# Four-layer graph network: another order in layer 2's loop, and its one-hot matrices made on ScalarE

## The chip, the cores and the metric

The kernel runs on one core of one Trainium2 chip. The metric is the device time of one execution in microseconds (us), given as the median of several runs. A profile of one further execution gives the times of single instructions. The engines are named as in the profile: PE is TensorE, PEld its weight loads, DVE is VectorE, ACT is ScalarE, POOL is GpSimd, and SP is the engine that issues most plain DMAs.

## The reference

There are 12500 nodes with 128 features and 212500 edges, sorted by destination. Four layers follow one another. Each normalises the node features, takes the positive part, gathers a row for the source of every edge, forms a message, sums the messages by destination and adds the result to the features. Layer 2, the third of them, is the one that changes. Its message is a tensor product of the source's features with nine numbers of the edge, cut to what matters:

```
PATHS = [(0, 0, 0), (0, 1, 1), (1, 0, 1), (1, 1, 0), (1, 2, 1)]
x1 = _split(features[src], IRREPS_IN)      # 32 scalars, 32 vectors of 3
x2 = _split(edge_sh, IRREPS_SH)            # 1 + 3 + 5 numbers an edge
for p, (i1, i2, io) in enumerate(PATHS):
    tmp = jnp.einsum('eui,ej,ijk->euk', x1[i1], x2[i2][:, 0, :], CG[p])
    msg = jnp.einsum('euk,uw->ewk', tmp, weights[p]) * alpha
    out_blocks[io] = msg if out_blocks[io] is None else out_blocks[io] + msg
...
return out.at[dst].add(msgs)
h = jnp.maximum(_layernorm(x, axis=-1), 0.0)
x = x + _L2_gnn_ref(h, edge_attr_9, edge_index, L2_gnn_weights)
```

## The kernel before

Edges are handled in groups of 1024: 8 slices (t = 0 to 7) of 128 edges, one edge to a partition, so that there are 208 groups (NG) in each layer. The destinations of a group lie within a window of 128 nodes. The sum over edges is a matmul: the message tile is the stationary operand and a one-hot tile is the moving one, with a 1 where edge and window node belong together. `rel` holds for every edge its destination's place in the window, 0 to 127, and `iop` holds 0 to 127 along the free dimension, in PSUM. The running sums stand in `acc`, features by nodes, in SBUF.

Layer 2 keeps an order written out by hand: under `tc.manual_schedule()` every engine executes its instructions in the order in which the program issues them, and semaphores only make them wait. One iteration of the loop takes one group g into the pipeline:

- `rows2` gathers the 8 slices of X from the table `htab` by 8 indirect DMAs, which POOL issues (L629 inside `gather`). X has 11 buffers.
- `mix(g + 1)` makes the edge factors Y ("harmonics") of the next group: a transposition on PE (L1129), its copy `eT` on ACT (L1131), a product with `mixer` on PE (L1132). Every fourth call also loads a batch of edge numbers `ef` through SP, and the last batch has a memset on POOL in it (L131).
- `window2` is a generator. Each `step(k)` drives group k's generator on to its next `yield`. The parts are: first A, the features times the first edge number, in 8 ACT instructions (L1142); second the one-hot S in one DVE instruction (L644 inside `one_hot`); third the products B and C in 8 DVE instructions (L1149 to L1161); fourth the sums `pag` over edges on PE in three blocks A, B and C (L1167), with two ACT copies to R (L1169, L1170); fifth the product `po` with the weights on PE (L1174); sixth the addition to `acc` on DVE (L1177).

Within iteration g the order is: `nodes.step`, gather g, A of g, `mix(g + 1)`, one-hot of g, addition of g-3, products of g, sums and copies of g-1, `po` of g-2. So ACT executes A(g), eT(g+1), R(g-1); PE executes the transposition and mixing of g+1, the sums of g-1, `po` of g-2; DVE executes the one-hot of g, the addition of g-3, the products of g.

`nodes` finishes blocks of 4 times 128 nodes (`node2`, 25 blocks) once their sums are complete: transpositions of `acc` on PE (L498), then normalisation on DVE and ACT, and stores through SP. They start at iteration `done + 4`, one iteration after the addition of the block's last group.

The matmuls are in float32, which the profile shows as two matmul and two weight-load instructions each: 16 for 8 slices.

Of the kernel before, what the change touches and what calls it, by code (L numbers as in the profile page):

```python
# [12 lines left out]
F = mybir.dt.float32  # L13
I = mybir.dt.int32
B16 = mybir.dt.bfloat16
AF = mybir.ActivationFunctionType
# [8 lines left out]
P = 128  # L25
T = 8
GE = P * T
W = 128
# [62 lines left out]
def gnn_kernel(ctx: ExitStack, tc, x, src, dst, ef16, ef9, ew, W0, We0, a0, lns, lnb, W1, b1,  # L91
# [6 lines left out]
    NG = NF + (tail > 0)  # L98
# [15 lines left out]
    vec, act, pool, pe = nc.vector, nc.scalar, nc.gpsimd, nc.tensor  # L114
# [59 lines left out]
    iop = cps.tile([P, W], F, name="iop")  # L174
# [3 lines left out]
    ones = cst.tile([P, P], F, name="ones")  # L178
# [294 lines left out]
    def node1(sp, pp, k):  # L473
        b0, nb = k * NBK, min(NBK, NB - k * NBK)
        xv = sp.tile([P, nb, D], F, name="xv")
        load_rows(xv, xtab[0], b0, nb)
        g = sp.tile([P, nb, P], F, name="g")
        act.activation(g.rearrange("p j n -> p (j n)"), acc[:, cols(k)], AF.Gelu_apprx_tanh)
        yield
        vec.memset(acc[:, cols(k)], 0.0)  # L480
        po = pp.tile([P, nb, D], F, name="pn")
        for j in range(nb):
            pe.matmul(po[:, j, :], g[:, j, :], W1T, start=True, stop=True)
        yield
        o = sp.tile([P, nb, D], F, name="o")
        vec.tensor_tensor(o, po, b1_b[:, None, :].to_broadcast([P, nb, D]), ALU.add)
        act.activation(o, o, AF.Gelu_apprx_tanh)
        yield
        vec.tensor_tensor(xv, xv, o, ALU.add)
        yield from keep(sp, 1, k, xv, True)  # L490
# [121 lines left out]
    class Nodes:  # L612
# [5 lines left out]
        def step(self, g):  # L618

            while self.next < NK and done[self.next] + self.delay <= g:  # L620
                self.going.append(self.make(self.next))
                self.next += 1
            self.going = [w for w in self.going if next(w, "end") != "end"]
            return self.going or self.next < NK
# [16 lines left out]
    def one_hot(sp, r, wgt=None, dt=F):  # L641
        s = sp.tile([P, T, W], dt, name="oh")
        if wgt is None:
            vec.tensor_tensor(s, iop[:, None, :].to_broadcast([P, T, W]), r[:, :, None].to_broadcast([P, T, W]),  # L644
                              ALU.is_equal)
        else:
            for t in range(T):
                vec.tensor_scalar(s[:, t, :], io, r[:, t : t + 1], wgt[:, t : t + 1], op0=ALU.is_equal, op1=ALU.mult)  # L648
        return s
# [109 lines left out]
    with (tc.tile_pool(name="e0", bufs=2) as sp, tc.tile_pool(name="e0p", bufs=2, space=PSUM) as pp,  # L759
# [106 lines left out]
        def spread_out(g):  # L866

            X, ev = xs.pop(g), alphas.pop(g)
            S = sp.tile([P, T, W], F, name="oh")
            vec.tensor_tensor(S, iop[:, None, :].to_broadcast([P, T, W]),  # L870
                              rel[:, g, :, None].to_broadcast([P, T, W]), ALU.is_equal)
# [5 lines left out]
            for t in range(T):  # L877
                pe.matmul(pag[:, 0, :], msg[:, t, :], S[:, t, :], start=t == 0, stop=t == T - 1)  # L878
            for t in range(T if g < G0 else 0):
                pe.matmul(pag[:1, 1, :], ones[:, :1], S[:, t, :], start=t == 0, stop=t == T - 1)  # L880

# [9 lines left out]
        with tc.manual_schedule():  # L891
# [4 lines left out]
            g = -1  # L896
# [193 lines left out]
    with (tc.tile_pool(name="e1", bufs=3) as sp, tc.tile_pool(name="e1p", bufs=2, space=PSUM) as pp,  # L1090
          tc.tile_pool(name="n1", bufs=2) as ns, tc.tile_pool(name="n1p", bufs=1, space=PSUM) as np_,
          tc.tile_pool(name="so", bufs=2) as ss, tc.tile_pool(name="sop", bufs=1, space=PSUM) as sps):
        reg = Window(DVE, True)
        S, pags, X = {}, {}, {}
        nodes = Nodes(lambda k: node1(ns, np_, k), 3)
        slots = Slots(ss, sps)
        with tc.manual_schedule():
            g = -1
            while nodes.step(g := g + 1) or g < NG + 2:
                if g < NG:  # L1100
                    X[g] = gather_apart(sp, htab[0], si[:, g, :], 12 * T)
                    S[g] = one_hot(sp, rel[:, g, :], eww[:, g, :])
                if 0 <= g - 2 < NG:
                    win = ds(reg.load(bi[0:1, g - 2 : g - 1]), W)
                    reg.end(vec.tensor_tensor(acc[:, win], acc[:, win], pags.pop(g - 2), ALU.add))  # L1105
                if 0 <= g - 1 < NG:
                    p = pags[g - 1] = pp.tile([P, W], F, name="pag")
                    s, r = S.pop(g - 1), X.pop(g - 1)
# [8 lines left out]
    def layer2(sp, pp, deep=4):  # L1117
        feats = feature_stream(ef9f, 9, 4, "ef", sp)

        def rows2(idx):  # L1120
            X = sp.tile([P, T, P], F, name="X", bufs=deep)
            gather(X, htab[1], idx)
            return X

        def mix(g):

            e = feats(g)
            py = pp.tile([P, 2, P], F, name="py")
            pe.transpose(py[: T * 9, 0, :], e, ident)  # L1129
            eT = sp.tile([T * 9, P], F, name="eT")  # L1130
            act.copy(eT, py[: T * 9, 0, :])  # L1131
            pe.matmul(py[:, 1, : T * NY], eT, mixer, start=True, stop=True)  # L1132
            return e.rearrange("p (t k) -> p t k", k=9), py[:, 1, : T * NY].rearrange("p (t k) -> p t k", k=NY)

        def stream2(g, idx, wgt):
            return rows2(idx), *mix(g)

        def window2(reg, got, r, b, nodes):
            X, e, Y = got
            A = sp.tile([P, T, P], F, name="A")  # L1140
            for t in range(T):
                act.activation(A[:, t, :], X[:, t, :], AF.Copy, scale=e[:, t, 0:1])  # L1142
            yield
            S = one_hot(sp, r)
            yield
            x1 = X[:, :, HD:].rearrange("p t (k u) -> p t k u", k=3)
            v3 = [P, T, 3, HD]
            B = sp.tile([P, T, 4, HD], F, name="B")
            vec.tensor_tensor(B[:, :, :3, :], X[:, :, None, :HD].to_broadcast(v3),  # L1149
                              Y[:, :, 0:3, None].to_broadcast(v3), ALU.mult)  # L1150
            V = pp.tile(v3, F, name="part", bufs=1)
            vec.tensor_tensor(V, x1, Y[:, :, 12:15, None].to_broadcast(v3), ALU.mult)  # L1152
            vec.tensor_reduce(B[:, :, 3, :], V.rearrange("p t k u -> p t u k"), AX.X, ALU.add)
            C = sp.tile(v3, F, name="C")
            part = pp.tile(v3, F, name="part", bufs=1)
            for i in range(3):
                o = part if i == 0 else sp.tile(v3, F, name="term", bufs=1)
                vec.tensor_tensor(o, x1[:, :, i : i + 1, :].to_broadcast(v3),  # L1158
                                  Y[:, :, 3 + 3 * i : 6 + 3 * i, None].to_broadcast(v3), ALU.mult)
                if i:  # L1160
                    vec.tensor_tensor(part if i == 1 else C, part, o, ALU.add)  # L1161
            yield
            pag = pp.tile([P, 3, W], F, name="pag", bufs=1)
            for c, f in enumerate((A, B, C)):
                for t in range(T):
                    lhs = f[:, t] if c == 0 else f[:, t].rearrange("p k u -> p (k u)")
                    pe.matmul(pag[: TPK[c] * HD, c, :], lhs, S[:, t, :], start=t == 0, stop=t == T - 1)  # L1167
            R = sp.tile([P, 3, W], F, name="R")
            act.copy(R[:, :2, :], pag[:, :2, :])  # L1169
            act.copy(R[: 3 * HD, 2, :], pag[: 3 * HD, 2, :])  # L1170
            yield
            po = pp.tile([P, W], F, name="po", bufs=1)
            for c, k in enumerate(TPK):
                pe.matmul(po, TP[: k * HD, c, :], R[: k * HD, c, :], start=c == 0, stop=c == 2)  # L1174
            yield
            win = ds(reg.load(b), W)
            reg.end(vec.tensor_tensor(acc[:, win], acc[:, win], po, ALU.add))  # L1177

        return rows2, mix, stream2, window2

    with (tc.tile_pool(name="e2", bufs=3) as sp, tc.tile_pool(name="e2p", bufs=2, space=PSUM) as pp,
          tc.tile_pool(name="n2", bufs=2) as ns, tc.tile_pool(name="n2p", bufs=1, space=PSUM) as np_):
        rows2, mix, _, window2 = layer2(sp, pp, 11)
        nodes = Nodes(lambda k: node2(ns, np_, k), 4)
        reg2, mixed, going = Window(DVE, True), {}, {}

        def step(k):
            if k in going:
                next(going[k], None)

        with tc.manual_schedule():
            mixed[0] = mix(0)
            g = -1
            while nodes.step(g := g + 1) or g < NG + 3:
                if g < NG:
                    going[g] = window2(reg2, (rows2(si[:, g, :]), *mixed.pop(g)), rel[:, g, :],
                                       bi[0:1, g : g + 1], widx[:, g : g + 1])
                    step(g)
                if g + 1 < NG:
                    mixed[g + 1] = mix(g + 1)  # L1200
                step(g)
                step(g - 3)
                step(g)
                step(g - 1)
                step(g - 2)

# [107 lines left out]
    with tc.tile_pool(name="l3", bufs=1) as lp:  # L1314
        stats = lp.tile([P, NK, 6], F, name="stats")
        with (tc.tile_pool(name="t3", bufs=1) as tp, tc.tile_pool(name="e3", bufs=2) as sp,
# [9 lines left out]
            X, S, sums, flat3, going = {}, {}, {}, {}, []  # L1326
# [3 lines left out]
            with tc.manual_schedule():  # L1330
# [9 lines left out]
                g, count, nk, alive = -1, 0, 0, True  # L1340
                while g < G0 + 8 or alive or going or waiting:
# [21 lines left out]
                    if 0 <= h < G0:  # L1363
                        p = sums[h] = pp.tile([P, 3 * P], F, name="pg")
                        s, r = S.pop(h), X.pop(h)
# [213 lines left out]
```

## Time and profile before

| | us |
|---|---|
| median of 3 runs | 10488.28 (10479.12 to 10490.92) |
| the profiled execution | 8214.33 |
| its span, first to last instruction | 8212.6 |
| layer 2 in it, about 4536 to 6841 | 2305 |

The profiled execution is shorter than the runs by 2274 us; nothing in the profile shows that time. The granted PE clock was 0.718 of full speed over the span.

To read the page: a group's line has source line, engine, operation, output and inputs with their shapes and count, then busy time and mean duration, then the idle time of the engine before the group's instructions, with what ended most of it. In a timeline line there are start, length, engine, source line, operation, count, and in brackets the idle time before it with its releaser. POOL's 8 gathers of a group are separate instructions.

### The profile page before, as it was taken

Reading aid. Unit: us, or ns where it says so; the run is one execution under the profiler, and the core shown is the slowest. Engines: PE = TensorE matmul, PEld = TensorE weight load, DVE = VectorE, ACT = ScalarE, POOL = GpSimd, SP = SyncE. Lnnn points to the kernel's source line nnn. Section 1 sums busy time; section 2 is a strip of 40 time slices with the busy share of each in tenths; the row PEclk is TensorE's granted clock in tenths of the full one; section 3 lists DMA queues with packets and bytes.
Section 4 is the critical chain, followed back from the end, with each engine's and each line's share of the span. In section 5 each row is a group of like instructions: output and inputs, shape, how many; then the busy total and the mean of one; then the engine's idle time right before and its main releaser. Section 6 shows DMA issues by size and latency. Waiting matters only on the chain. (4 is left out here: it accounts for less than half of the span.)

```text
span 8212.6 us, 100482 instructions
## 1 busy us (share of the span) xinstructions
PE 5336.5 (65%) x32201; PEld 3954.0 (48%) x32202; DVE 5348.6 (65%) x10674; ACT 1691.6 (21%) x4403; POOL 5718.1 (70%) x6026
## 2 busy tenths in 40 slices
PE   3455555544446666666666677777777775877786
PEld 2344444444434444444444677777777772222222
DVE  6466666666666666556562788888888883444444
ACT  2011111111110000000000223222322221444443
POOL 0677777777747777777777677777766745777773
PEclk8677787756555555555555788888888886888988
DMA  5544444444422222222222222222222214444444
GB/s 85 102 107 107 109 109 106 110 107 108 107 60 57 65 61 64 62 61 65 61 63 62 59 66 69 65 66 66 63 64 60 64 44 119 108 107 108 107 108 111
DMA packets 719228, 675.69 MB, mean 82 GB/s; under 512 B 342845, under 2 KB 596298, under 8 KB 718667
## 3 DMA queue, kind: packets, MB, share of 16 engines
q0 software_dynamic: 207552, 427.14, 21.2%
q1 hardware_dynamic: 511136, 242.04, 11.8%
q8 instruction: 255, 4.18, 0.2%
q14 instruction: 285, 2.33, 0.1%
HBM read 606.24 MB, written 63.30 MB: 82 GB/s over the span
## 5 line engine op out<-in xcount | busy, mean ns | idle before, releaser
L629 POOL DMA_INDIRECT X<-htab,si x1664 | 1574.4, 946 | 606.5 <-issue 571.0
L637 POOL DMA_INDIRECT X<-htab,si x1664 | 1583.6, 952 | 560.1 <-issue 251.1
L629 POOL DMA_INDIRECT X<-tab,si x1664 | 1599.1, 961 | 507.4 <-issue 486.4
L1110 PE MATMUL pag<-oh,X 128*128 128x128 f32 x3328 | 1236.7, 483 | 729.2 <-DMA X<-htab,si 694.9
L1110 PEld LDWEIGHTS pag<-oh,X 128*128 128x128 f32 x3328 | 808.8, 306 | 1138.8 <-DMA X<-htab,si 1059.2
L637 POOL DMA_INDIRECT X<-tab,si x968 | 919.6, 950 | 374.4 <-issue 134.0
L878 PE MATMUL pag<-oh,msg 128*128 128x128 f32 x3328 | 673.7, 384 | 636.1 <-DVE msg L873 636.1
L878 PEld LDWEIGHTS pag<-oh,msg 128*128 128x128 f32 x3328 | 622.0, 288 | 656.8 <-DVE msg L873 656.8
L1167 PE MATMUL pag<-oh,A 128*128 128x128 f32 x3328 | 660.1, 382 | 0.0
L1289 ACT CAST xb<-px 128x384 bf16<-128x384 f32 x1050 | 501.3, 478 | 677.2 <-PE px L1278 662.6
L1167 PEld LDWEIGHTS pag<-oh,A 128*128 128x128 f32 x3328 | 639.0, 295 | 0.4 <-ACT R L1170 0.4
L1368 PE MATMUL pg<-X,oh 128*128 128x384 bf16 x968 | 357.8, 373 | 268.4 <-DVE f L1361 149.9
L644 DVE TENSOR_TENSOR oh<-iop,rel 128x1024 f32<-128x1024 f32 (+1 forms) x321 | 389.4, 1213 | 209.1 <-PE pg L1368 201.9
L1142 ACT ACTIVATE A<-X,ef 128x128 f32<-128x128 f32 x1664 | 509.8, 393 | 11.8 <-DMA X<-htab,si 11.8
L1105 DVE TENSOR_TENSOR acc<-acc,pag 128x128 f32 x208 | 59.4, 285 | 646.0 <-PE pag L1110 597.8
L1132 PE MATMUL py<-mixer,eT 72*128 72x120 f32 x416 | 130.1, 405 | 531.5 <-ACT eT L1131 531.5
L1167 PE MATMUL pag<-oh,B 128*128 128x128 f32 x3328 | 466.8, 300 | 0.0
L1167 PEld LDWEIGHTS pag<-oh,B 128*128 128x128 f32 x3328 | 461.2, 221 | 0.0
L648 DVE TENSOR_SCALAR oh<-io,rel,eww 128x128 f32<-128x128 f32 x1664 | 445.5, 355 | 3.9 <-PE pag L878 3.9
L1278 PE MATMUL px<-tabS,oha 128*32 128x384 bf16 x4326 | 410.7, 367 | 0.2
L1169 ACT COPY R<-pag 128x256 f32<-128x256 f32 x208 | 77.4, 372 | 1567.3 <-PE pag L1167 1567.3
L1158 DVE TENSOR_TENSOR term<-X,py 128x768 f32<-128x768 f32 x416 | 395.1, 950 | 7.1
(402 smaller groups left out, 8714.7 us busy)
## 6 DMA issues: line engine op xcount, KB each, us to landing
rb<-rel SPq DMA_DIRECT2D x208, 256.0 KB
X<-htab,si POOLq DMA_INDIRECT x3328
X<-tab,si POOLq DMA_INDIRECT x2632
lob<-lo SPq DMA_DIRECT2D x126, 224.0 KB
xtab<-xv SPq DMA_DIRECT2D x72, 256.0 KB
xv<-xtab SPq DMA_DIRECT2D x72, 256.0 KB
ef<-in_edge_attr_dram SPq DMA_DIRECT2D x51, 256.0 KB
htab<-t SPq DMA_DIRECT2D x48, 256.0 KB
```

The lines of the kernel that those rows point to most:

```text
L629: pool.indirect_dma_start(out=t[:, s, :], out_offset=None, in_=table[:, :], in_offset=bass.IndirectOffsetOnAxis(ap=idx[:, s : s + 1], axis=0))
L637: pool.indirect_dma_start(out=ts[-1], out_offset=None, in_=table[:, :], in_offset=bass.IndirectOffsetOnAxis(ap=idx[:, s : s + 1], axis=0))
L644: vec.tensor_tensor(s, iop[:, None, :].to_broadcast([P, T, W]), r[:, :, None].to_broadcast([P, T, W]), ALU.is_equal)
L648: vec.tensor_scalar(s[:, t, :], io, r[:, t : t + 1], wgt[:, t : t + 1], op0=ALU.is_equal, op1=ALU.mult)
L878: pe.matmul(pag[:, 0, :], msg[:, t, :], S[:, t, :], start=t == 0, stop=t == T - 1)
L1110: pe.matmul(p, r[t], s[:, t, :], start=t == 0, stop=t == T - 1)
L1142: act.activation(A[:, t, :], X[:, t, :], AF.Copy, scale=e[:, t, 0:1])
L1158: vec.tensor_tensor(o, x1[:, :, i : i + 1, :].to_broadcast(v3), Y[:, :, 3 + 3 * i : 6 + 3 * i, None].to_broadcast(v3), ALU.mult)
L1167: pe.matmul(pag[: TPK[c] * HD, c, :], lhs, S[:, t, :], start=t == 0, stop=t == T - 1)
L1278: pe.matmul(px[q * SL : (q + 1) * SL, :], a[:, jj * P + q * SL : jj * P + (q + 1) * SL], tabS[:, blk, :], start=True, stop=True)
L1289: act.copy(x[:, : 3 * P], px)
L1368: pe.matmul(p, s[:, t, :], r[t], start=t == 0, stop=t == T - 1)
```

## The change

In the loop, `mix(g + 1)` goes to the front of the iteration, ahead of gather g and A(g). The one-hot no longer has a step of its own: it is issued at the beginning of the first step, on ACT, ahead of A. It is made in two passes. The first takes for each slice the absolute value of `iop - rel` (8 instructions, with `-rel` as the bias, one number a partition), and the second takes the positive part of 1 minus that, over all 1024 columns at once. For whole numbers this is 1 where the two are equal and 0 elsewhere. `far` holds `-rel`, one small ACT instruction a group. With one `yield` less, the second `step(g)` is now the products, and the addition of g-3 comes behind them.

```diff
         def window2(reg, got, r, b, nodes):
             X, e, Y = got
+
+            far = sp.tile([P, T], F, name="far")
+            act.mul(far, r, -1.0)
+            off = sp.tile([P, T, W], F, name="off", bufs=1)
+            for t in range(T):
+                act.activation(off[:, t, :], iop, AF.Abs, bias=far[:, t : t + 1])
+            S = sp.tile([P, T, W], F, name="oh")
+            act.activation(S, off, AF.Relu, bias=ones[:, :1], scale=-1.0)
             A = sp.tile([P, T, P], F, name="A")
             for t in range(T):
                 act.activation(A[:, t, :], X[:, t, :], AF.Copy, scale=e[:, t, 0:1])
-            yield
-            S = one_hot(sp, r)
             yield
...
             while nodes.step(g := g + 1) or g < NG + 3:
+                if g + 1 < NG:
+                    mixed[g + 1] = mix(g + 1)
                 if g < NG:
                     going[g] = window2(reg2, (rows2(si[:, g, :]), *mixed.pop(g)), rel[:, g, :],
                                        bi[0:1, g : g + 1], widx[:, g : g + 1])
                     step(g)
-                if g + 1 < NG:
-                    mixed[g + 1] = mix(g + 1)
                 step(g)
                 step(g - 3)
-                step(g)
                 step(g - 1)
                 step(g - 2)
```

The order of the engines becomes: ACT eT(g+1), one-hot(g), A(g), R(g-1); PE as before; DVE products(g), addition(g-3).

## The prediction

> **What bounds the kernel now.** I first read the table by stages, then for layer 2 the waits, one iteration of the timeline, and two counts of gathers against groups consumed.
>
> The table by stages (length, then busy time and instruction count of PE, PEld, DVE, ACT, POOL, then granted PE clock, DMA share and GB/s):
>
> ```profile
> core 0: us, PE busy (x) PEld busy (x) DVE busy (x) ACT busy (x) POOL busy (x), PEclk, DMA share, GB/s
> 4540.00:6820.00 2280.00, 1717.00 (x11939) 1660.04 (x11940) 1950.15 (x2491) 672.75 (x2379) 1571.93 (x1663) 0.83 0.23 61
> ```
>
> Layer 2 is 2280 us for 208 groups, 10.96 us each. No engine's busy time fills it; ACT is the emptiest at 30%. So the question is who waits for whom. The waits of layer 2's middle 2000 us (waiting, releaser, total, times, longest):
>
> ```profile
> ACT R L1169 <- PE pag L1167: 1382.6, 183, 9.3
> POOL X L629 <- issue: 512.4, 1410, 2.7
> ...
> PE py L1132 <- ACT eT L1131: 463.5, 182, 4.6
> DVE acc L1177 <- PE po L1174: 195.6, 123, 3.8
> ```
>
> ACT waits for PE's sums, and PE waits for ACT's eT, once in each group: a ring. The timeline of one iteration shows it in order:
>
> ```profile
> 5042.70 0.37 ACT L1169 COPY R<-pag 128x256 f32<-128x256 f32 x1 [7.58 <-PE pag L1167]
> ...
> 5043.13 2.45 ACT L1142 ACTIVATE A<-X,ef 128x128 f32<-128x128 f32 x8
> ...
> 5045.48 0.25 ACT L1131 COPY eT<-py 72x128 f32<-72x128 f32 x1
> ...
> 5045.78 0.78 PE L1132 MATMUL py<-mixer,eT 72*128 72x120 f32 x2 [2.38 <-ACT eT L1131]
> ...
> 5046.35 3.32 PE L1167 MATMUL pag<-oh,A 128*128 128x128 f32 x16
> ...
> 5049.51 1.95 PE L1167 MATMUL pag<-oh,B 128*128 128x128 f32 x16
> ...
> 5053.30 0.37 ACT L1169 COPY R<-pag 128x256 f32<-128x256 f32 x1 [7.57 <-PE pag L1167]
> ```
>
> From R to R is 10.60 us. Within it PE stands 2.38 us, because eT is queued behind eight A's (2.45 us) that PE doesn't need yet. The ring is R 0.43, A 2.35, eT 0.30, mixing 0.57 to the first sum, sums about 6.95.
>
> POOL is the second limit. A gather is 0.946 us and the next starts 0.30 us after it. Gathers issued, and ACT's A's done (8 of each are one group), in two stretches:
>
> ```profile
> 4700.00:5700.00 1000.00, 753.43 (x795) 0.83 0.26 67
> 5850.00:6700.00 850.00, 575.51 (x609) 0.83 0.23 61
> ```
>
> ```profile
> 4700.00:5700.00 1000.00, 222.39 (x728) 0.83 0.26 67
> 5850.00:6700.00 850.00, 189.20 (x620) 0.83 0.23 61
> ```
>
> In the first stretch POOL does 795 gathers, 1.258 us each, 10.06 us a group; ACT takes in only 91 groups, 10.99 each. POOL gets ahead until the 11 buffers of X are full, and in the second stretch follows the consumers (1.396 us a gather). So now the ring paces layer 2, and POOL has 0.9 us a group of slack and no more.
>
> **What the skill says.** In the Trainium skill, "ScalarE: Activation LUTs", section "What ACT_TABLE_LOAD costs", an ACTIVATE with a per-partition operand takes about 280 ns + 0.833 ns a column, one with immediates 186 ns, and neighbours overlap by 93 ns. The trace agrees: A, 128 columns with a pointer scale, is 393 ns against 387, and eight take 2.45 us, 0.306 each. The same page, "Table sets: the hidden batching unit", says that cheap functions, relu, copy and abs among them, are in every set, so that no table switch is due; the trace of before has no Abs and can't confirm it. "TensorE: Matmul & The Clock Gate", section "Part 1: The HAM clock gate (the "warmup" mystery)", says that an idle PE falls to half clock and needs some 3.4 us of work to come back. The trace fits: 16 sums of A behind the 2.38 us wait take 3.32 us, 16 of B right behind 1.95.
>
> **The change part by part**, against the profiled 8214.33 us.
>
> *mix(g+1) first.* PE passes nothing with it, since gather, A and one-hot have no PE instruction: its order stays. On SP the `ef` load of every fourth group passes no other DMA. On POOL the one memset passes eight gathers (its wait for A was 17.7 us; with POOL no longer far ahead it shrinks; worth nothing by itself, as X's buffers were full there). On ACT eT passes the eight A's. The ring becomes R, eT, mixing, sums: 10.60 - 2.35 = 8.25 us, and less if PE, waiting less, keeps its clock. The one-hot and A run beside the sums of g-1.
>
> *One-hot on ACT.* Added each group: `far` about 0.2 us (8 columns; nearest row 0.297 for `rs`); 8 Abs with a pointer bias, taken as A's 2.45 us. Reading PSUM instead of SBUF may cost less or more: R's copy from PSUM, 96 columns, is 264 ns, and without any overlap 8 x 0.393 = 3.14, so 2.1 to 3.2. The Relu over 1024 columns by the skill's price is an estimate of 280 + 853 = 1133 ns (the row t<-h, 512 columns with immediates, 635 ns measured against 612 priced), 1.1 to 1.3. Sum 3.78 us. ACT's own work before is 2.45 + 0.25 + 0.37 + 0.26 = 3.33, so 7.1 us a group (6.7 to 8.2), plus a mean 0.3 of node work. That is below 10.06. What waits behind it on ACT is R(g-1): eT(g+1), one-hot and A take 0.25 + 3.78 + 2.45 = 6.5 us, while PE needs 0.57 + 6.95 = 7.5 for the same interval. So R isn't late; with warm sums of 5.7 they are level.
>
> *One-hot off DVE.* Removes 208 x 1.213 = 252 us of DVE. Left: 8 products x 0.954 = 7.63, addition 0.29, node work about 0.6 (22 blocks' rows sum to some 112 us over 183 groups): 8.5 us a group. DVE wasn't the bound; this pays only by keeping DVE under POOL.
>
> *Addition behind the products.* The products no longer wait for `po` (195.6 us in 183 groups, 1.07 each), and the addition finds `po` long done. The price: at 25 block starts PE's transpositions of `acc` (L498) need the addition that is now the last DVE work of the iteration before, and the eT chain and sums are queued behind them on PE. That delays PE by up to the products' 7.6 us less what it would have waited for C anyway; I take 5 us, 25 x 5 = 125 us or 0.6 a group (0 to 0.9). It is covered by X's buffers as long as ring plus 0.6 stays under POOL's 10.06: 8.85, yes.
>
> *Sum.* Ring 8.85, DVE 8.5, ACT 7.4, PE's own work with a cold clock about 9.3 (0.3 + 0.8 + 7 + 0.8 and hand-overs), all under 10.06. POOL then paces layer 2 from its first gather at 4536.5: 1664 x 1.258 = 2093 us, the last ends at 6630 instead of 6718.5, its rows land some 2.8 us later (as at the stage's start) and A(207) ends near 6633 instead of 6810. What follows A(207) takes as long as before: products 7.6 and the last sums. Gain 177 us; I take 170 for a few stretches in which the consumers fall behind. Profiled execution about 8044 us.
>
> **The profile and the median.** The median 10488.28 is 2274 us above the profiled 8214.33, and no view says where. I take that part as untouched: 10488 - 170 = 10318. Were it spread evenly, the gain would scale by 1.277 to 217: 10271.
>
> **The rivals.**
>
> *Gathers are slower in the runs than in the profile.* The 2274 us over the program's 5960 gathers are 0.38 us each; a group would then take 8 x 1.63 = 13.0 us on POOL, above the ring's 10.6, so layer 2 would be POOL's already and gain only some 0 to 20 us at its end: 10478. For it: POOL is nearly gapless in layers 0 and 2 of the profile, so a slower POOL would add up unhidden. Against: the same instructions show 0.946 us throughout the trace.
>
> *The sums are slower in the runs.* If PE's clock there is lower, the ring is longer before and POOL hides less: up to the whole 2.35 x 208 = 490 us; 10140 as a middle. Against: the trace's other layers are POOL's, so a slow PE alone hardly makes 2274 us.
>
> *ACT becomes the bound: slower.* If Abs or Relu lies outside the loaded table set, each group pays two switches on ACT, by the skill's 2.66 us (estimate from "ScalarE: Activation LUTs") 5.3 us: 7.1 + 5.3 = 12.4 us a group, 208 x 12.4 = 2580 instead of 2280, 10790. It decides from where ACT passes 10.96 us a group, 3.6 above my sum. A part-way form, passes much dearer than priced, goes the same way. Against: Copy, Relu and Sqrt already alternate here and A's durations stay 384 to 411 ns.
>
> *The edit has no hold:* if C's products on DVE already end last before the sums, the ring won't shrink. Against: C ends at 5050.86 while its sums start at about 5051.3, a near thing in that iteration, but DVE's own chain is 1.2 us shorter after.
>
> **The numbers.** Main case 0.62 (10265 to 10365); gathers slower 0.15, mostly within 0.2%; sums slower 0.10; ACT the bound 0.11; no hold 0.02. A measurement of this kernel can tell about 0.2%, 21 us, from no change. Faster 0.62 + 0.10 + 0.03 = 0.75; same 0.13; slower 0.12. The time is the main case's, 10318. The range takes in the slower-gather case and stops short of a larger gain or a loss: 10200 to 10500.
>
> **What would show it.** Right: gathers at 1.25 to 1.26 us each through all of layer 2, ACT's A waiting for X's landing, PE's wait for eT mostly gone, ACT busy about 1460 us in the stage, 16 sums of A nearer 2 us where PE doesn't wait, the last gather near 6630. Wrong: gathers still paced by buffers, or Abs above 400 ns a piece, or long waits of PE at L498 behind the addition, or a profile shorter by 170 us beside a median that hasn't moved.

## The result, and the profile after

The changed kernel takes 10508.89 us (median of 11 runs, 10494.18 to 10536.59), the kernel before in the same runs 10487.37 (11 runs, 10457.59 to 10505.23): ratio 1.0026 [1.0015, 1.0037]. It is a quarter of a per cent slower, where 10318 was forecast. Its profiled execution took 10521.42 us (span 10519.6), as long as the runs.

One plain fact is needed to read everything below. The runs were made in sets, each on one chip, and there are two kinds of sets: the kernel before takes 8216 to 8228 us on chips 4, 6 and 12 (12 in two sets) and 10477 to 10624 us on chips 5, 7 and 15. The profile of before, 8214 us, is of the first kind, the timed runs above are of the second. The kinds are called **8200 chips** and **10500 chips** here, and a ratio is always taken within one set. That it is the chip that makes the kind is likely but not shown: no chip was seen in both kinds, yet only one was seen twice.

The lines of after that answer to those of before. Layer 2 in the table by stages (length, then busy time and count of PE, PEld, DVE, ACT, POOL, then PE clock, DMA share, GB/s):

```profile
5461.00:8664.00 3203.00, 1944.14 (x11954) 1707.36 (x11954) 1727.27 (x2324) 1400.28 (x4468) 1572.39 (x1666) 0.72 0.17 46
```

3203 us against about 2300. DVE has lost some 220 us, its one-hots, and ACT gained some 730 (252 and 786 were forecast), but no engine comes near the length of the stage. POOL's 1572 us are those of before: a gather still takes 0.945 us. The waits of layer 2's middle (waiting, releaser, total us, times, longest):

```profile
POOL X L629 <- ACT A L1150: 933.6, 93, 11.8
ACT R L1175 <- remote: 822.4, 60, 14.7
DVE acc L1183 <- PE po L1180: 654.7, 95, 12.6
PEld pag L1173 <- issue: 645.6, 620, 2.6
PE pag L1173 <- issue: 578.9, 643, 2.5
```

Before, the longest wait in this list was 9.3 us. Now POOL stands 10 us at a time for A, ACT and DVE stand up to 14.7 us for sums and products, and PE itself stands "issue" at 1263 of its loads and matmuls: it waits for nothing that the profile shows, in the middle of a row of sums. ("remote" means that a semaphore ended the wait, but that the profile finds no instruction that gave it; by the program, R waits for the sums on PE.) One such cycle in the timeline:

```profile
7011.52 0.94 POOL L629 DMA_INDIRECT X<-htab,si  x1 [10.71 <-ACT A L1150]
...
7012.74 0.37 ACT L1175 COPY R<-pag 128x256 f32<-128x256 f32 x1 [1.50 <-PE pag L1173]
...
7017.74 1.58 PE L1173 MATMUL pag<-oh,C 128*96 128x128 f32 x13
...
7020.04 0.38 PE L1173 MATMUL pag<-oh,C 128*96 128x128 f32 x2 [0.72 <-issue]
...
7022.16 0.37 PE L1173 MATMUL pag<-oh,C 128*96 128x128 f32 x1 [1.75 <-issue]
...
7029.17 0.37 PE L1129 MATMUL py<-ident,ef 128*72 128x128 f32 x1 [1.51 <-issue]
7030.24 0.94 POOL L629 DMA_INDIRECT X<-htab,si  x1 [0.30 <-issue]
7034.29 0.37 ACT L1175 COPY R<-pag 128x256 f32<-128x256 f32 x1 [14.67 <-remote]
...
7034.72 0.27 ACT L1131 COPY eT<-py 72x128 f32<-72x128 f32 x1
7034.87 0.22 ACT L1142 ACTIVATE far<-rel 128x8 f32<-128x8 f32 x1
...
7035.12 2.17 ACT L1145 ACTIVATE off<-iop,far 128x128 f32<-128x128 f32 x8
...
7037.33 1.15 ACT L1147 ACTIVATE oh<-off,ones 128x1024 f32<-128x1024 f32 x1
...
7038.38 2.43 ACT L1150 ACTIVATE A<-X,ef 128x128 f32<-128x128 f32 x8
...
7041.08 0.94 POOL L629 DMA_INDIRECT X<-htab,si  x1 [9.89 <-ACT A L1150]
```

From 7011.52 to 7030.24 POOL issues 16 gathers without a pause. The first group's sums run at full speed (13 matmuls in 1.58 us, at 7017.74). Then, some 8 us into the burst, single matmuls come 0.7 to 2 us apart, and R, which needs sums that started by 7022.16, begins at 7034.29. That is 12.1 us after the last sum has started, and 3.1 us after the last gather has ended. POOL had stopped because the 11 buffers of X were full. Now ACT runs R, eT, one-hot and A; A's end frees a buffer, and POOL starts the next burst at 7041.08.

Worked out from the trace over all of layer 2: POOL's bursts are 94 times 16 gathers, with 97 pauses of 10.6 us between them (1031 us in all); in 72 groups R begins more than 3 us after the last C matmul has started (median of these 6.4 us), and where POOL has paused by then, the median is 3.1 us after POOL's last gather. There are 94 stretches with four or more slow weight loads; the middle 80% of them begin 7.7 to 8.8 us after the burst's first gather. The counts of gathers and of A's move together now, as in this stretch (8 are a group; 1000 us take 66 groups, 15.1 us each):

```profile
5700.00:6700.00 1000.00, 502.60 (x532) 0.73 0.17 45
```

```profile
5700.00:6700.00 1000.00, 160.41 (x528) 0.73 0.17 45
```

### The profile page after: what moved, and what is told of

It is laid out like the page before. It is cut to its first block, busy times and chain, and to the rows that moved or that the text cites. A ratio compares the mean times of both kernels' runs of the same rounds, so it can differ in the third digit from the quotient of the medians.

```text
span 10519.6 us, 101846 instructions
## 1 busy us (share of the span) xinstructions
PE 5280.2 (50%) x32201; PEld 3921.8 (37%) x32202; DVE 5122.4 (49%) x10466; ACT 2415.6 (23%) x6483; POOL 5707.7 (54%) x6026
## 5 line engine op out<-in xcount | busy, mean ns | idle before, releaser
L1110 PE MATMUL pag<-oh,X 128*128 128x128 f32 x3328 | 709.9, 379 | 494.2 <-issue 271.4
L878 PE MATMUL pag<-oh,msg 128*128 128x128 f32 x3328 | 726.1, 406 | 391.8 <-DVE msg L873 275.7
L1173 PE MATMUL pag<-oh,C 128*96 128x128 f32 x3328 | 576.7, 292 | 635.8 <-issue 633.8
L1110 PEld LDWEIGHTS pag<-oh,X 128*128 128x128 f32 x3328 | 640.0, 284 | 679.3 <-issue 437.3
L1173 PEld LDWEIGHTS pag<-oh,C 128*96 128x96 f32 x3328 | 438.3, 172 | 706.8 <-issue 704.9
L803 PE MATMUL pt<-WeB,eT 128*128 128x32 f32 x416 | 112.1, 358 | 1064.6 <-ACT eT L801 746.7
L1183 DVE TENSOR_TENSOR acc<-acc,po 128x128 f32 x208 | 59.4, 286 | 1172.1 <-PE po L1180 698.4
L1173 PE MATMUL pag<-oh,A 128*128 128x128 f32 x3328 | 566.1, 342 | 0.0
L1173 PEld LDWEIGHTS pag<-oh,A 128*128 128x128 f32 x3328 | 548.4, 257 | 0.1
L803 PEld LDWEIGHTS pt<-WeB,eT 128*128 128x128 f32 x416 | 86.2, 259 | 1133.3 <-ACT eT L801 789.5
L648 DVE TENSOR_SCALAR oh<-io,rel,eww 128x128 f32<-128x128 f32 x1664 | 446.7, 354 | 18.7 <-issue 14.7
```

What stands on the lines that cost most here:

```text
L1110: pe.matmul(p, r[t], s[:, t, :], start=t == 0, stop=t == T - 1)
```

## The experiments

Length of each layer in the traces, from its first gather to the next layer's first (us), with R to R, the mean time of a group in layer 2, and POOL's pauses over 1 us there ("rest" is what follows layer 2):

| kernel (chip) | layer 0 | layer 1 | layer 2 | rest | R to R | pauses: number, us |
|---|---|---|---|---|---|---|
| before, first profile | 2197 | 2107 | 2304 | 1372 | 10.9 | 52, 103 |
| changed, after_2 (12) | 2196 | 2110 | 2117 | 1374 | 10.0 | 0 |
| before, control_3 (7) | 2842 | 2442 | 3233 | 1873 | 14.9 | 152, 1052 |
| changed, after_3 (15) | 2784 | 2430 | 3199 | 1845 | 14.7 | 97, 1024 |
| order alone, order_only_2 (15) | 2785 | 2425 | 2955 | 1858 | 13.5 | 186, 798 |
| changed, no gathers, after_nog (5) | 2784 | 2430 | 1859 | 1856 | 8.3 | 0 |
| before, no gathers, before_nog (5) | 2772 | 2428 | 2354 | 1854 | 10.7 | 0 |

### The two edits apart, on an 8200 chip

control is the kernel before, unaltered.

> The kernel of before, unchanged, for a second trace. Theory S (PE is short of instructions): the profile of the changed kernel shows PE starting one instruction each 0.70 us for stretches of 4 to 14 us, about one stretch in 256 PE instructions, with no wait in sight; the 8214 us profile of before shows none. If that is the usual state of both kernels, this trace has a span near 10490 us, the same stretches, and a layer 2 of about 3150 to 3200 us, against 3203 in the changed kernel. Rival R (the stretches come with the change): a span near 8214 us or a layer 2 near 2300 us, with no such stretches in it.

8229.51 us beside 8225.2 (9 runs, 8211 to 8234): the set of runs is one like the first profile.

order_only keeps the one-hot on DVE, between A and the products (diffs are against the changed kernel, where nothing else is said):

```diff
-            far = sp.tile([P, T], F, name="far")
-            act.mul(far, r, -1.0)
-            off = sp.tile([P, T, W], F, name="off", bufs=1)
-            for t in range(T):
-                act.activation(off[:, t, :], iop, AF.Abs, bias=far[:, t : t + 1])
-            S = sp.tile([P, T, W], F, name="oh")
-            act.activation(S, off, AF.Relu, bias=ones[:, :1], scale=-1.0)
...
+            yield
+            S = one_hot(sp, r)
             yield
...
                     step(g)
                 step(g)
+                step(g)
                 step(g - 3)
```

> Only the order changes: mix(g+1) first and the addition behind the products, one-hot still on DVE. Theory S: PE's supply paces layer 2, so taking ACT's A out of the ring is worth little: ratio 0.995 to 1.002. Rival A (the change's two halves cancel: the order gains what the ScalarE one-hot loses): ratio 0.985 or lower, 150 us or more gained.

8034.21 us, ratio 0.9769 [0.9756, 0.9782]; layer 2 falls to 2122 us. On this chip the order alone brings all there is.

onehot_only keeps the old order of the loop and takes the new one-hot:

```diff
-                if g + 1 < NG:
-                    mixed[g + 1] = mix(g + 1)
                 if g < NG:
...
                     step(g)
+                if g + 1 < NG:
+                    mixed[g + 1] = mix(g + 1)
-                step(g)
                 step(g - 3)
+                step(g)
```

> Only the one-hot moves to ScalarE, with the old order (A with the one-hot ahead of eT of the next group). ACT then has 3.5 us more inside the ring. Theory S as such: if ACT's instructions fit into times in which PE is short of instructions anyway, ratio 1.00 to 1.01. If the ring R, one-hot, A, eT, mixing, sums still counts in the usual state, 208 x 3.5 = 730 us longer at most, ratio up to 1.07. Rival A wants 1.015 or more here together with 0.985 or less for the order alone.

9020.01 us, ratio 1.0968 [1.0953, 1.0983]; layer 2 takes 3093 us. Its waits:

```profile
PE py L1132 <- ACT eT L1131: 1091.3, 183, 6.3
```

PE waits 6.0 us for eT in each group (1091.3 in 183), 2.5 in the profile before (463.5 in 182): with eT behind A, the one-hot's 3.5 us stand in the ring as well. The loss of 795 us is more than the 730 at most that was expected; R to R grew by 3.8 us, and where the last 0.3 come from isn't shown. So on this chip the one-hot is free only where eT has gone ahead of it.

few_c leaves the C sums of seven of eight slices out of the changed kernel:

```diff
-                for t in range(T):
+                nt = 1 if c == 2 else T
+                for t in range(nt):
...
-                    pe.matmul(pag[: TPK[c] * HD, c, :], lhs, S[:, t, :], start=t == 0, stop=t == T - 1)
+                    pe.matmul(pag[: TPK[c] * HD, c, :], lhs, S[:, t, :], start=t == 0, stop=t == nt - 1)
```

> The changed kernel with the sums of block C made for one slice of eight only: 28 of 114 PE instructions a group fewer, 5824 in all (this leaves out seven eighths of the C sums, so the values differ). Theory S: the time follows PE's instruction count; layer 2 falls by about a quarter of 3203 us, 600 to 800 us, ratio 0.925 to 0.945. Rival P (POOL, ACT or DVE bounds layer 2, and PE's slow stretches only fill a wait): at most 100 us, ratio 0.99 or more. Rival W (only the sums' own 1.7 us a group count): 350 us, ratio about 0.967.

8031.03 us, ratio 0.9765 [0.975, 0.978], no better than with all sums: PE isn't the bound here.

### The changed kernel itself on that chip

> The changed kernel, unchanged, once more. Where PE is fully supplied (the kernel before near 8220 us): the forecast sum holds, POOL paces layer 2 and the time is 8030 to 8050 us, ratio 0.976 to 0.979, as in the order-only and few-C runs. Where PE starts single instructions 0.70 us apart in stretches (the kernel before near 10490): 10500 to 10520, ratio 1.001 to 1.004, layer 2 near 3200 us.

> The kernel of before, unchanged, beside the changed kernel. If its time is near 10490 us: theory S expects stretches of single PE instructions 0.70 us apart in all layers, and a layer 2 of 3150 to 3200 us, as long as the changed kernel's; the rival (they come with the change) expects none. If its time is near 8220 us: no such stretches, layer 2 near 2300 us.

The changed kernel takes 8030.47 us, ratio 0.9764 [0.9751, 0.9778], and the unaltered kernel before 8217.87 beside 8225.57. The gathers in 1000 us of layer 2 of after_2:

```profile
4700.00:5700.00 1000.00, 756.25 (x800) 0.87 0.26 68
```

800 gathers, 1.25 us each, without a single pause: POOL paces layer 2 and the profiled execution is within 0.2% of the 8044 of the prediction's sum. The last gather ends at 6617.5 us, where 6630 was forecast. **The forecast mechanism is right on the 8200 chips.** The rest is about the others.

### A 10500 chip: fewer sums, fewer gathers

> The kernel of before, unchanged. Near 8220 us it adds nothing. Near 10490 us, theory S expects in layer 2 the stretches of single PE instructions 0.70 us apart, and a layer 2 of 3150 to 3200 us where the fully supplied PE takes 2305.

10624.12 us beside 10624.25: the kernel before has the long layers too, all four of them (table). In its layer 2 ACT stands up to 20.2 us for R, where 9.3 was the longest in the first profile:

```profile
ACT R L1169 <- remote: 916.3, 53, 20.2
```

few_c_2 is few_c again, and half_gather gathers X for even groups only, so that an odd group uses its neighbour's rows:

```diff
-                    going[g] = window2(reg2, (rows2(si[:, g, :]), *mixed.pop(g)), rel[:, g, :],
+                    X2 = rows2(si[:, g, :]) if g % 2 == 0 else X2
+                    going[g] = window2(reg2, (X2, *mixed.pop(g)), rel[:, g, :],
```

> The changed kernel with the sums of block C for one slice of eight only (seven eighths of C's sums left out): 28 of 114 PE instructions a group fewer. With PE supplied: 8030, as before, since POOL paces. Near 10490 for the kernel before: theory S, layer 2 shorter by 600 to 800 us, ratio 0.925 to 0.945; rival P (something other than PE's supply paces layer 2 there), ratio 0.99 or more.

> The changed kernel with X gathered for every second group only and used twice (half of layer 2's gathers left out, so the values differ). With PE supplied, theory P (POOL paces the changed kernel's layer 2 at 10.06 us a group): the next bound takes over, ring, DVE or PE at 8.5 to 9.3 us a group, 160 to 320 us less than the changed kernel's 8030: 7710 to 7870. If POOL isn't the bound: 8000 or more. With PE short of instructions (kernel before near 10490), theory S: no gain, within 1% of the changed kernel.

few_c_2: 10531.12 us, ratio 0.9906 [0.9882, 0.993], layer 2 still 3149 us. Theory S, that PE is short of instructions as such, falls: 2912 matmuls and as many weight loads fewer change little. Nor does the trace show that PE's instructions are loaded too slowly: the packets of the two DMA queues of the kind "instruction" take 0.98 us (q8) and 0.35 us (q14) in after, 0.99 and 0.41 in after_2 (medians), and the slow stretches of after begin anywhere from 0.1 to 33 us behind a packet of q8. Which queue serves PE the profile doesn't say. half_gather: 9555.69 us, ratio 0.8989 [0.8967, 0.9011]; layer 2 falls to 2174 us, some 1030 below after's; the 832 gathers left out would take 1040 us at 1.25 each. POOL still pauses 91 times for 11.4 us, 1041 us in all, as long in sum as with twice the gathers (1031). This fits theory E (PE's work doesn't complete while POOL gathers), which the next runs test.

### Without gathers, and with fewer buffers

after_nog and before_nog gather for the first 11 groups of layer 2 only; later groups use those rows again. deep3 is the changed kernel with 3 buffers of X instead of 11. The first diff is that of after_nog, and before_nog has the same lines in the kernel before; the second is deep3's.

```diff
+        held2 = {}
...
-                    going[g] = window2(reg2, (rows2(si[:, g, :]), *mixed.pop(g)), rel[:, g, :],
+                    if g < 11:
+                        held2[g] = rows2(si[:, g, :])
+                    going[g] = window2(reg2, (held2[g % 11], *mixed.pop(g)), rel[:, g, :],
```

```diff
-        rows2, mix, _, window2 = layer2(sp, pp, 11)
+        rows2, mix, _, window2 = layer2(sp, pp, 3)
```

> The changed kernel with X gathered for the first 11 groups only and used again after that (197 of 208 groups' gathers left out, so the values differ). Theory E (where the kernel before takes about 10500, PE's matmuls don't complete while POOL gathers without a pause, and come free about 3.15 us after POOL's last gather): without gathers layer 2 falls from 3203 us to what ring, DVE and PE need, 8.5 to 9.5 us a group, 1800 to 1980 us, and there is no sum whose copy to R comes over 3 us late. Rival S (PE is short of instructions whatever POOL does): 2900 us or more in layer 2. Where the kernel before takes about 8220: 1800 to 1980 us in layer 2 as well, against 2117 with the gathers.

> The kernel of before with the same gathers left out. Theory E: the ring alone remains, 10.6 to 11.0 us a group, layer 2 of 2200 to 2300 us wherever it runs, so that the change's gain without gathers is 250 to 450 us on either kind of run. Rival S, where the kernel before takes about 10500: 2900 us or more, and no gain.

> The changed kernel with 3 buffers of X instead of 11, so that POOL can run no more than 2 groups ahead. Where the kernel before takes about 8220: POOL still paces, 8030 to 8080. Where it takes about 10500, theory E: PE's stops depend on how many gathers come without a pause; with the buffers full for most of layer 2 both depths let POOL run about two groups at a time, so within 1% of the changed kernel; a clear gain (2% or more) would say that POOL's lead itself does the harm.

after_nog: 9160.79 us, ratio 0.8729 [0.8704, 0.8753]. before_nog: 9655.28, ratio 0.9207 [0.9182, 0.9232]. deep3: 10456.69, ratio 0.9976 [0.9965, 0.9987], with the same pauses (102, 1061 us in all), so the depth of X isn't the cause. Without gathers the hold-ups of layer 2 are gone, and the change is worth 495 us of it (1859 against 2354; 250 to 450 was expected, and 2300 at most for before_nog). The longest wait of after_nog and the longest three of before_nog in a stretch of 1200 us:

```profile
PEld py L1132 <- ACT eT L1131: 118.1, 144, 2.1
```

```profile
ACT R L1169 <- PE pag L1167: 832.7, 112, 8.9
PEld py L1132 <- ACT eT L1131: 306.7, 112, 3.2
PE py L1132 <- ACT eT L1131: 277.4, 112, 2.9
```

In before_nog the ring of the prediction stands bare (R to R 10.68 us, PE waiting for eT in each group); in after_nog it is gone. What paces after_nog, 8.28 us a group, is DVE, busy 1462.67 of 1500 us:

```profile
5700.00:7200.00 1500.00, 1288.51 (x10330) 1213.60 (x10329) 1462.67 (x1998) 1216.83 (x3864) 0.16 (x1) 0.95 0.07 19
```

### Which part of a gather it is, and which edit costs the gain

Four kernels ran on one 10500 chip, beside 10488.47 us for the kernel before (19 runs). after_3 is the changed kernel and order_only_2 the kernel of order_only. plain_x loads X by plain DMAs from SP's queue, the same number, bytes and rows of 512 B, but from consecutive rows of the table (first diff; the loop's call gains the argument g). pool_busy is after_nog with 8 memsets on POOL in place of a group's gathers (second diff, against after_nog).

```diff
-        def rows2(idx):
+        def rows2(idx, g=None):
...
-            gather(X, htab[1], idx)
+            if g is None:
+                gather(X, htab[1], idx)
+            else:
+                for s in range(T):
+                    b = (g * T + s) % (N // P) * P
+                    nc.sync.dma_start(X[:, s, :], htab[1][b : b + P, :])
```

```diff
                     if g < 11:
                         held2[g] = rows2(si[:, g, :])
+                    else:
+                        for s in range(T):
+                            pool.memset(sp.tile([P, 1024], F, name="junk", bufs=1), 0.0)
```

> The changed kernel, unaltered, as the base for the three runs beside it. If the kernel before takes about 8220 us in this set, about 8030 (ratio 0.976); if it takes about 10500, ratio 0.99 to 1.005 with layer 2 near 3200 us.

> The changed kernel, with X of layer 2 loaded by 1664 plain DMAs from SyncE's queue (128 rows of 512 B each, consecutive rows of the table instead of the source nodes' rows: other rows, so another result) instead of POOL's 1664 gathers. Same bytes in the same pieces, into the same tiles. Theory G (POOL's own gathers hold PE up): layer 2 is freed as without gathers, about 8.3 us a group, 1860 us or a little more if SyncE's issue limits it, which in a set with the kernel before at about 10500 is ratio 0.87 to 0.90. Theory D (the DMA traffic into X holds PE up, whoever starts it): layer 2 stays near 3000 to 3200 us there, ratio 0.98 to 1.0. In a set with the kernel before at about 8220 both say about 7780 to 7850, ratio 0.95.

> The changed kernel with gathers for the first 11 groups of layer 2 only (the later groups use those rows again, so another result), and 8 memsets of 128 x 1024 on POOL in each later group in place of 8 gathers; the memsets wait for nothing but each other. Theory P (POOL being busy, whatever it does, holds PE up): layer 2 goes back to 2500 us or more in a set with the kernel before at about 10500. Theory G (it is the gathers): near the 1860 us without gathers, ratio about 0.873, unless the memsets themselves take longer than 8.3 us a group, when POOL's own sum sets it.

> The order of the changed kernel alone (next harmonics first, addition behind the products), with the one-hot still made by VectorE. In a set with the kernel before at about 10500: if the small loss of the changed kernel (ratio 1.0026 there) comes from ScalarE's two passes, this one is at 0.985 to 1.0 and below the changed kernel; if from the order, at 1.0 to 1.005, the same. In a set with the kernel before at about 8220: 0.977, the same as the changed kernel.

| | us | ratio | layer 2 |
|---|---|---|---|
| after_3 | 10511.9 | 1.0024 [1.0014, 1.0034] | 3199 |
| plain_x | 9372.73 | 0.8947 [0.8926, 0.8968] | 2055 |
| pool_busy | 9180.61 | 0.8763 [0.8744, 0.8782] | 1875 |
| order_only_2 | 10262.36 | 0.9793 [0.9773, 0.9813] | 2955 |

**plain_x** moves the same bytes into X and is freed: theory D, that the bytes moved hold PE up whoever starts them, falls. Its layer 2 is some 180 to 200 us longer than those of pool_busy and after_nog, for another reason: DVE now waits for X to land (217.3 us in 1500). The list of DMA issues shows the exchange:

```profile
X<-htab SPq DMA_DIRECT2D x1664, 64.0 KB
...
X<-htab,si POOLq DMA_INDIRECT x1664
```

1664 plain DMAs of 64 KB have taken the place of half of the X<-htab gathers; those that remain belong to layer 1. **pool_busy** keeps POOL busy 89% of the time (1332.9 of 1500 us in layer 2's middle; 8 memsets of 0.952 us a group) and is freed as well: theory P falls. So on these chips it is POOL's gathers that hold PE up, not the bytes and not a busy POOL. In the Trainium skill, "DMA: Bandwidth & Descriptors", section "SWDGE vs HWDGE vs iDMA", the descriptors of a DMA issued from GpSimd are computed by software running there, and those of SyncE's by a hardware block. The profile names the queues in that way: plain_x moved the bytes of X from q0 "software_dynamic" (427 MB before, 318 after) to q1 "hardware_dynamic" (242, then 351). Three things changed together there: who makes the descriptors, the rows (scattered or consecutive), and the packets (by the queues' totals 32 for a gather, 144 for a plain DMA of the same 64 KB). Which of them holds PE up, no run here tells.

**order_only_2** is the surprise. On the same chip the order alone gains 226 us, more than was expected of it, and the changed kernel has lost them again. The difference of 250 us between the two is what moving the one-hot to ACT costs, which on the 8200 chip had cost nothing. The waits of order_only_2 in layer 2's middle, and a pause of its timeline:

```profile
POOL X L629 <- ACT A L1142: 667.9, 164, 8.8
```

```profile
6241.73 0.37 ACT L1169 COPY R<-pag 128x256 f32<-128x256 f32 x1 [8.79 <-remote]
6241.96 0.94 POOL L629 DMA_INDIRECT X<-htab,si  x1 [0.30 <-issue]
...
6244.60 0.26 ACT L1131 COPY eT<-py 72x128 f32<-72x128 f32 x1 [1.80 <-remote]
6244.76 2.45 ACT L1142 ACTIVATE A<-X,ef 128x128 f32<-128x128 f32 x8
...
6247.48 0.94 POOL L629 DMA_INDIRECT X<-htab,si  x1 [4.58 <-ACT A L1142]
...
6254.56 0.37 ACT L1169 COPY R<-pag 128x256 f32<-128x256 f32 x1 [7.34 <-PE py L1129]
...
6260.26 0.95 POOL L629 DMA_INDIRECT X<-htab,si  x1 [3.09 <-ACT A L1142]
```

Here A stands right behind eT, and POOL goes on 2.9 us after eT's start (6244.60 to 6247.48); in the changed kernel 6.4 us (7034.72 to 7041.08), the one-hot's 3.5 us more. POOL has a beat of one group here: 180 bursts of 8 gathers and 186 pauses of 4.3 us. PE is still held up, but less: R typically begins 1.9 us after its last sum has ended (0.04 in after_2), and at 6241.73 and 6254.56 it begins while POOL still gathers. A burst of 8 lasts 9.7 us, hardly longer than the 8 us after which PE slows in after; a burst of 16 lasts 19.7. I read it so: with the long pause PE finishes its group meanwhile, the next A frees buffers before the burst is over, and 16 gathers run in one, which lets the hold-up grow to 10 us and more. The pauses add up to 1024 us in after_3 and 798 here; that is 226 of the 244 us by which layer 2 differs.

### A before the one-hot

If that reading is right, the eight A's ahead of the one-hot should give both: the order's gain, and DVE relieved.

```diff
+            A = sp.tile([P, T, P], F, name="A")
+            for t in range(T):
+                act.activation(A[:, t, :], X[:, t, :], AF.Copy, scale=e[:, t, 0:1])
             far = sp.tile([P, T], F, name="far")
...
             act.activation(S, off, AF.Relu, bias=ones[:, :1], scale=-1.0)
-            A = sp.tile([P, T, P], F, name="A")
-            for t in range(T):
-                act.activation(A[:, t, :], X[:, t, :], AF.Copy, scale=e[:, t, 0:1])
```

> The changed kernel with one thing swapped on ScalarE: the eight A's of a group before its one-hot instead of behind it. In a set with the kernel before at about 10490, where the order alone gave 0.979 and the changed kernel 1.0024. Theory L (the one-hot's 3.5 us ahead of A delay the release of X's buffer, so that POOL's pause is 10 us once in two groups instead of about 4 in each, and two groups' gathers run in one burst): POOL pauses in each group again, R to R goes back from 14.7 to about 13.5 us, layer 2 from 3200 to about 2950, ratio 0.975 to 0.985. Theory W (it is ScalarE's added work as such, 3.5 us a group, wherever it stands): R to R stays near 14.7, ratio 0.995 to 1.005. In a set with the kernel before at about 8220 the ratio is 0.976 in both, since POOL's gathers pace it.

> The same kernel as a_first, in another set of runs. If the kernel before takes about 10490 here: theory L (A's place behind the one-hot) R to R about 13.5 us, layer 2 about 2950, ratio 0.975 to 0.985; theory W (ScalarE's added work wherever it stands) R to R about 14.7, ratio 0.995 to 1.005. If the kernel before takes about 8220, 0.978 again and nothing is told apart.

Both sets were on 8200 chips (6 and 4): 8030.13 us beside 8215.58, ratio 0.9779 [0.9763, 0.9796], and 8039.28 beside 8228.4, ratio 0.9771 [0.9754, 0.9787]. There POOL has no pause and the two theories give the same, so this experiment doesn't decide. That the one-hot costs its 250 us by standing ahead of A is thus read from the timelines and not shown; that the one-hot costs them is.

## Why the prediction was wrong, point by point

**The step that failed** is the last: "no view says where. I take that part as untouched", with the 170 us of the profiled execution subtracted from the median. The layers' table shows where the 2274 us lay: in all four layers, and in layer 2 some 900 us of it. (On chip 15, 10488 less the other layers of its traces and 232 us ahead of the first gather leaves about 3190 us for layer 2 of the kernel before, an estimate, beside the changed kernel's 3199.) The stage that the change is about was another one in the runs, with other waits: 14.7 to 14.9 us a group, gathers and pauses, in both kernels. In that stage one term of the sum, the one-hot on ACT, taken as hidden under POOL's time, cost 250 us.

The order alone gained 226 us there, where the whole change was forecast at 170. That these are near each other is luck: the forecast mechanism is a POOL that gathers without a pause, and there it paused 186 times. A profiled execution 22% below the median should have been taken as a sign that the profile and the runs may differ in mechanism, and the chance of the main case lowered for it.

**The ring** of the kernel before was right: 10.60 us in the profile before, 10.68 without gathers. That the changed kernel without gathers takes 8.28 us a group where the ring was forecast at 8.25 is chance: DVE paces it (forecast at 8.5), and the ring only has to be shorter. How much shorter, no run shows.

**POOL as the next bound at 10.06 us a group** was right on the 8200 chips, and with it the 8044: 8030. (The 14 us between are mostly gathers 1.25 us apart instead of 1.258, times 1664. The sign named for it, A waiting for X to land, didn't come; DVE's B waits, 227.8 us in 1700.) On the 10500 chips the assumption under it fails, that PE works on undisturbed while POOL gathers. A group costs its gathers plus the pause in which PE catches up, 10.06 and about 5 us, in both kernels.

**The one-hot on ACT costed at nothing.** The size was good: 3.78 us forecast; 0.22, 2.17 and 1.15 us, together 3.5, measured. The eight Abs are cheaper than A's 2.45, which they were taken as. In the Trainium skill, "ScalarE: Activation LUTs", section "Table sets: the hidden batching unit", abs and relu are in every set; the trace now agrees as far as it can, since Abs, Relu and A follow one another without a gap, and the rival "ACT becomes the bound" is out: ACT is busy 44% of layer 2. But the cover for these 3.5 us was POOL without a pause. Where POOL pauses for A, they lie in the pause (7034.72 to 7041.08 above), and what they cost without that cover wasn't asked: 250 us, more than the gain of the order.

**The one-hot off DVE** was said to pay only by keeping DVE under POOL. It wasn't even needed for that: order_only, with the one-hot on DVE, is as fast on the 8200 chip. Where gathers don't pace the layer it would pay: in after_nog DVE is the bound, and 1.21 us of one-hot more would make its 8.28 us about 9.5, an estimate, that is half of the 495 us gained there.

**The addition behind the products** was charged at L498, 5 us a block. In after_2 no wait at L498 for the addition is to be seen; PE waits at `po` instead, for the addition to release it (PEld po 249.7 us, 122 times, in 1700 us), and POOL's time hides it, as it was to hide the other.

**The rivals.** "Gathers are slower in the runs" named the right suspect and came nearest in time (10478), yet with another mechanism: a gather takes 0.945 us in the runs as well, and it is PE that suffers. It would also have given the order alone nothing, and the order gained 226 us. "The sums are slower in the runs" is not what the trace shows: where PE isn't held up, 13 matmuls still take 1.58 us. "No hold" rests on a misreading: the C product that ends about when the sums of 5051.29 start is the next group's. The one that they need ended at 5040.86, 10.4 us earlier, so DVE was far from ending last.

**What stays open:** why POOL's gathers hold PE up on chips 5, 7 and 15 and not on 4, 6 and 12; what in a gather does it; why the one-hot on ACT costs 250 us there, by its place ahead of A or by its length; and so whether a_first keeps the order's gain. Of the kernels with the full result, order_only is the one that was measured faster than the kernel before on both kinds of chips, 0.9769 and 0.9793.

## What to carry to other kernels

When a profile's own time is far from the median of the runs, compare the stages of a profile taken under the runs' conditions before costing anything, since another bound may rule there. Work that is free under a saturated engine can be on the path as soon as that engine pauses: ask of each added instruction whether it stands ahead of the one that releases the next buffer (here a reading of the timelines, not yet tested). Where two edits come together, measure each alone; here one gained 2.1% and the other lost it.

## What was not expected of the hardware

While POOL issues 16 indirect gathers back to back (0.945 us each, 0.30 between), PE slows after about 8 us to one instruction every 0.7 to 2 us on some chips. In the cycle shown ACT begins 12.1 us after the last sum that it needs has started, and 3.1 us after the last gather has ended. The same bytes by plain DMAs from SyncE (layer 2 at 2055 us) and a POOL busy with memsets (1875 us) do nothing of the sort, against 3199 us with the gathers. And it is not there in every set of runs: the kernel before takes 8216 to 8228 us on three chips and 10477 to 10624 us on three others.
